# Moving transposes and row sums behind the value matmuls in a two-block diffusion transformer kernel

## The chip, the core and the metric

The kernel runs on one core of a Trainium2 chip. The metric is the device time of one execution in microseconds; the median of three runs is given. One further execution was taken with the hardware profiler. Engines are named as in the profile: PE is the matmul engine, PEld its weight loads, DVE, ACT and POOL the vector, scalar and general engines, SP the engine that issues most DMAs.

## The reference, cut to what matters

Everything is float32. Eight samples of 512 tokens with 256 features pass through two transformer blocks. Block 0 has 16 heads of 16 features and no projections in its self-attention:

```python
h = modulate(ln(x), shift_sa, scale_sa)
q = ln(_heads(h, H)) * qn_w + qn_b
k = ln(_heads(h, H)) * kn_w + kn_b
v = _heads(h, H)
attn = jax.nn.softmax(jnp.einsum('bhqd,bhkd->bhqk', q, k) * scale, axis=-1)
x = x + gate_sa[:, None, :] * _unheads(jnp.einsum('bhqk,bhkd->bhqd', attn, v))
```

A cross-attention over 64 context tokens and a gated feed-forward (256 to 1024 and back) follow. Block 1 has 16 heads of 64 features, with projections `wq`, `wkv`, `wo`, rotary positions on queries and keys, then a cross-attention over the same context and a GELU feed-forward:

```python
attn_in = _adaln(x, cond, ln1_w, ln1_b, g1_w, g1_b, b1_w, b1_b)
x = _attn(attn_in, attn_in, sa_wq, sa_wkv, sa_wo, sa_bo) + x
cross_in = _adaln(x, cond, ln1_w, ln1_b, g1_w, g1_b, b1_w, b1_b)
x = _attn(cross_in, ctx_n, ca_wq, ca_wkv, ca_wo, ca_bo) + x
x = gelu(ffn_in @ ff_w1 + ff_b1) @ ff_w2 + ff_b2 + x
```

## The kernel before, in words

**Order.** Inside the two stages that the change touches, the order of instructions on PE, DVE, ACT and POOL is the order in which the program writes them (a manual schedule). Semaphores between engines follow from the tiles. So "behind the values" means: later in the program, and later on each engine's queue.

**Block 0.** `run_blocks` walks a list of blocks, 18 for each sample (`CYCLE = H + 2`). In a sample's cycle, 16 blocks are self-attention: four head groups `g`, each with four key tiles `kt`; the two others (places `X0 = 11` and `X1 = 13`) are the previous sample's cross-attention. A block has scores (four matmuls on four 32-row strips of PE, into two tiles of `bank_s`, then two exponentials on ACT, L590) and values (four matmuls on four 32-column strips; plain values of a self-attention block go to `ps_O`). From block 18 on, blocks come in pairs. For the pair (i, i+1) the loop writes:

```python
scores(i)
others(i - 2); others(i - 1)
scores(i + 1)
values(i - 1); values(i)
```

`others` runs what was filed under a block's number in `beside` with `at(i, fn)`; below, it is called the middle. Filed there are:
- `queries_keys(g)` (L564 on): four 128x128 transposes of the normed heads `z` into one bank (L570), copied to `q` by ACT (L573) and to `k` by DVE (L574); filed 4 blocks before the group's first scores (2 in the first cycle).
- `group_end(g)`: ACT copies `ps_O` to `oT` (L603). `group_back(g)`: four transposes of `oT` into one bank (L610); DVE reads the denominators, inverts them and multiplies (L617 to L619); POOL multiplies by the gate and adds to x (L621, L622).
- `turn` of `batch2` (cross-attention) and of `batch3` (feed-forward): `transposed` (L427, L428) writes eight transposes into two banks, and ACT turns each into half of `hT`.
- The feed-forward's `up` (two matmul pairs into two banks; tanh on ACT L779; two DVE operations L780, L781) and `down`, the cross-attention's queries and its output projection, and the norms (DVE, with powers on POOL).

Turns of the feed-forward are collected in a list `later` and filed last, so that they come behind the other work of the same block number. All matmul outputs of the middle take a bank from `bank_x`, which in block 0 rotates over three banks (two of `ps_X` and `ps_D`). Each PE matmul of the program is two in the trace [...]; a transpose is one.

**Block 1's self-attention.** `slots` walks slots `m`, each with two blocks of 32-row scores. A slot writes: scores of block 2m+1; the jobs of `steps[m]`, the middle again, with the entry of `mid[m]` put in at place 1; scores of block 2m+2; values of blocks 2m and 2m+1 (64-column matmuls into `ps_O` and `ps_D`); then the list `after[m]`. A sample has eight slots: four head groups of four key tiles. `bank_x` rotates over two banks here. Jobs in the middle are projections for queries and keys (two banks each, rotated by DVE L999, L1000 and added on POOL L1002, L1003), for values (two banks, copied by ACT L989), the output projection `out_tiles` (one bank, added to x by DVE L464), and `turn` of the next sample.

The softmax denominators: POOL and DVE add the exponentials of a head group (L1035, L1039) into `sm`; `sums(g)` reduces `sm` with four 32-column matmuls by `ones32` into one bank, ACT copies it to `den` (L1055), DMAs carry it to DRAM and back reshaped into `rec`; `inverse(g)` is a DVE reciprocal (L1067) and two more DMA steps that broadcast it into `rb`; `scaled(g)` is two POOL products `oT * rb` (L1085). With n = 8b + 2g + 2, `sums` is in the middle of slot n (`mid[n]`), `inverse` in `after[n]`, `scaled` last in the middle of slot n+1. `out_tiles(0)` and `out_tiles(1)` come first in the middles of slots 8b + 10 and 8b + 11. The next sample's `turn` is the last job of the slot that holds the sums of g = 1.

Of the kernel before, what the change touches and what calls it, by code (L numbers as in the profile page):

```python
# [17 lines left out]
B, N, D, H, T, CD, FF = 8, 512, 256, 16, 64, 192, 1024  # L18
# [30 lines left out]
        self.scores, self.values = scores, values  # L49


def run_blocks(blocks, beside, alone):

    def scores(i):
        for fn in blocks[i].scores if i < len(blocks) else []:
            fn()

    def values(i):
        for fn in blocks[i].values if 0 <= i < len(blocks) else []:
            fn()

    def others(i):
        for fn in beside.get(i, []):
            fn()

    others(-1)
    for i in range(alone):  # L70
        scores(i)
        values(i - 1)
        others(i)
    scores(alone)
    values(alone - 1)
    for i in range(alone + 1, max(len(blocks) + 2, *(k + 3 for k in beside)), 2):
        scores(i)
        if i > alone + 1:
            others(i - 2)
        others(i - 1)  # L80
        scores(i + 1)
        values(i - 1)
        values(i)


def fast_path(ctx: ExitStack, tc: tile.TileContext, a: dict, out: bass.AP):
# [394 lines left out]


    blocks = []
    beside = {}

    def at(i, fn):
        beside.setdefault(max(i, -1), []).append(fn)

    CYCLE = H + 2
    X0, X1 = 11, 13  # L490
# [2 lines left out]
    def batch1(b):  # L493
        s = {}
        base = CYCLE * b
# [128 lines left out]
        n = 0  # L624
        for g in range(4):
            for kt in range(NT):
                while n in (X0, X1):
                    n += 1
                i = base + n
                blocks[i] = block(g, kt)  # L630
                if g == 0 and kt == 0:
                    if b == 0:
                        def before():
                            for n in range(3):
                                norm(n)
                            nc.vector.tensor_copy(qk_cols, cols[:, 0:2])
                            for fn in (first_modulated, head_centre, head_square, head_var):
                                fn(0, 0)
                            head_scale(0, 0, nc.vector)

                        at(-1, before)
                        at(0, lambda: awake(3))
                        for k, par, fns in ((0, 1, (first_modulated, head_centre)),
                                            (1, 1, (head_square, head_var, head_scale)), (2, None, (first_modulated,)),
                                            (3, None, (head_centre,)), (4, None, (head_square, head_var, head_scale))):
                            for fn in fns:
                                at(k, lambda fn=fn, par=par: fn(0 if par else 1, par))
                        at(5, lambda: spread(s["gate"], b, G_SA, D))
                    else:

                        for m, k in enumerate((-11, -10, -9) if b == 1 else (-13, -12, -10)):
                            at(i + k, lambda m=m: norm(m))
                        for c in range(2):
                            for k, fn in zip((-6, -5, -5, -4) if b == 1 else (-7, -5, -3, -3) if c else (-9, -8, -7, -7),
                                             (head_centre, head_square, head_var, head_scale)):
                                at(i + k, lambda c=c, fn=fn: fn(c))
                if kt == 0:
                    at(i - (2 if i <= CYCLE else 4), lambda g=g: queries_keys(g))
                if kt == NT - 1:
                    at(i + 1, lambda g=g: group_end(g))  # L660
                    at(i + 2 + (b > 0 and n % 2 == 0), lambda g=g: group_back(g))
                n += 1


    def batch2(b):
        s = {}
        base = CYCLE * (b + 1)
# [67 lines left out]

        for n, i in enumerate((2, 2, 3)):
            at(base + i, lambda n=n: prepare(n))
        at(base + 5, turn)
        at(base + 7, lambda: queries(0))
        at(base + 8, lambda: queries(1))  # L740
        end = b == B - 1
# [9 lines left out]
    def batch3(b):  # L751
        s = {}

        base = CYCLE * (b + 2) + {B - 3: 4, B - 2: 3, B - 1: -2}.get(b, 0)

        def prepare(n):

            if n == 0:
                s["gate"] = gate = wk3.tile([P, D], F32, tag="gate3", name="gate3")
                spread(gate, b, G_FF, D)  # L760
                s["pieces"] = normed_in_pieces(wk2, b, EPS0, lambda z: s.update(z=z))
            s["pieces"][n]()

        def turn():
            s["hT"] = transposed(wk2, s["z"], b, modT[:, 6:8, :], modT[:, 4:6, :])

        def up(f):
            if f == 0:
                s["hid"] = wk3.tile([P, 8, N], F32, tag="hid", name="hid", bufs=1)
            fs = slice(f * P, (f + 1) * P)  # L770
            pss = []
            for w in (w_1, w_3):
                ps = bank_x()
                for k in range(2):
                    mm(ps, w[:, k, fs], s["hT"][:, k, :], k == 0, k == 1)
                pss.append(ps)

            t = wk3.tile([P, N], F32, tag="t", name="t")
            nc.scalar.activation(t, pss[0], AF.Tanh, scale=0.5)  # L779
            nc.vector.scalar_tensor_tensor(t, t, 1.0, pss[0], ALU.add, ALU.mult)  # L780
            nc.vector.tensor_tensor(s["hid"][:, f, :], pss[1], t, ALU.mult)  # L781

        def down(t):
            ps = bank_x()[:, 0:D]
            project_tile(ps, 0, lambda k: s["hid"][:, k, :], w_2, 8, t)
            tmp = wk2.tile([P, 2, D], F32, tag="tmp", name="tmp", bufs=1)[:, 0, :]
            nc.vector.tensor_tensor(tmp, ps, s["gate"], ALU.mult)
            x = xs[b][:, t, :]
            nc.vector.tensor_tensor(x, x, tmp, ALU.add)

        places = {B - 2: (3, 3, 5, 6, 8), B - 1: (2, 2, 2, 4, 7)}.get(b, (4, 4, 6, 8, 9))
        for n in range(3):
            at(base + places[n], lambda n=n: prepare(n))
        later.append((base + places[3], turn))
        for f in range(8):
            at(base + places[4] + f, lambda f=f: up(f))
        for t in range(4):
            at(base + places[4] + 8 + (t if b > B - 3 else 2 * t), lambda t=t: down(t))

    blocks = [Block([], []) for _ in range(CYCLE * (B + 2))]  # L800
# [120 lines left out]
    later = []  # L921
    for b in range(B):
        batch2(b)
        batch3(b)
    for i, fn in later:
        at(i, fn)
    run_blocks(blocks, beside, CYCLE)
    ms.close()
    l0.close()

# [34 lines left out]
    with tc.tile_pool(name="ph4", bufs=2) as wk:  # L965
# [5 lines left out]
        def last(slot, fn):  # L971
            steps.setdefault(slot, []).append(fn)

        def batch4(b):
# [115 lines left out]
            if b:  # L1090

                pieces = normed_in_pieces(nk, b, EPS1, lambda z: s.update(z=z))
                last(base - 8, pieces[0])
                last(base - 6, pieces[1])
                after[base - 6] = [pieces[2]]
                last(base - 5, lambda: add_row(b, row("sabo")))
                last(base - 4, turn)
                last(base - 3, lambda: queries(0))
                last(base - 2, lambda: values(0, (0, 1)))
                last(base - 2, lambda: keys(0))  # L1100
                last(base - 1, lambda: values(0, (2, 3)))
            else:
                s["hT"] = ready

                def begin():
                    queries(0)
                    add_row(0, row("sabo"))
                    both = bank_s()
                    keys(0, (both[:, 0, :], both[:, 1, :]))
                    values(0, (0, 1))  # L1110
                    values(0, (2, 3))

                last(-1, begin)
                last(4, lambda: [nc.gpsimd.memset(z, 0.0) for z in (kb, vb)])
                last(5, lambda: load_kb(0))
# [9 lines left out]
        for b, (score, value, sums, inverse, scaled, out_tiles, _) in enumerate(todo):  # L1125
            base = 2 * NG * b
            for g in range(NG):
                if b == B - 1 and g == NG - 1:
                    break
                n = base + 2 * g + 2  # L1130
                mid[n] = lambda g=g, f=sums: f(g)
                after.setdefault(n, []).append(lambda g=g, f=inverse: f(g))
                last(n + 1, lambda g=g, f=scaled: f(g))
            if b < B - 1:
                for qp in range(2):
                    steps[base + 2 * NG + 2 + qp].insert(0, lambda qp=qp, f=out_tiles: f(qp))

        def slots():
            n = B * NG * NT
# [1129 lines left out]
```

## Time and profile before

| | us |
|---|---|
| Runs: median (lowest to highest of 3) | 2404.46 (2400.79 to 2407.53) |
| Profiled execution, its own time | 2400.53 |
| Its span, from first to last instruction | 2398.4 |
| PE busy | 2373.4 (99%) |
| PEld, DVE, ACT, POOL busy | 1160.7, 1138.7, 890.6, 967.9 |
| Start of block 1's self-attention slots | about 866 |
| One cycle of block 0 (18 blocks), e.g. 316.8 to 402.2 | 85 |
| One sample of block 1's self-attention, e.g. 1244.2 to 1366.8 | 122.5 |

The granted clock of PE was 0.998 of full speed. Busy time is from an instruction's start to its end, and instructions of an engine can overlap, so mean durations are longer than the distance from start to start. A timeline row merges instructions of one line and tile that follow without a gap; "x8" is their number; what stands in brackets is the idle time before the row and who ended it.

### The profile page before, as it was taken

The page shows a single profiled execution, that of the slowest core. Times are in us where ns is not written, and L with a number is a line of the kernel's source. Part 1 is how long each engine was busy: PE and PEld are TensorE (multiplying, and loading weights), DVE is VectorE, ACT ScalarE, POOL GpSimd, SP SyncE. Part 2 cuts the span into 40 slices and gives each one's busy share as a digit, 9 for nine tenths or more (in the row PEclk, how much of TensorE's full clock was granted, in tenths as well). Part 3 has the DMA queues.
Part 4 walks back from the last instruction along what each step waited for, and adds up shares of the span by engine and source line. Part 5 has one row for each costly group of instructions (what it writes and reads, how often), then busy time and mean ns, then how long its engine had stood idle before and what let it go on. Part 6 is the DMA issues. An engine that isn't in the chain of part 4 may idle for free.

```text
span 2398.4 us, 28561 instructions
## 1 busy us (share of the span) xinstructions
PE 2373.4 (99%) x10964; PEld 1160.7 (48%) x10964; DVE 1138.7 (47%) x2115; ACT 890.6 (37%) x1118; POOL 967.9 (40%) x588
## 2 busy tenths in 40 slices
PE   9999999999999999999999999999999999999998
PEld 4333544544545633444444444444445566667665
DVE  4564534434335345554545464645435767651110
ACT  4665545555542134333333333333332222221221
POOL 4563223323201046554646455555553544541110
PEclk9999999999999999999999999999999999999999
DMA  5130000000002001000000000000113222210000
GB/s 185 33 108 11 16 15 9 17 16 7 13 11 92 1 1 32 10 28 10 28 10 19 19 19 19 19 19 19 36 55 106 69 69 69 65 56 31 18 22 20
DMA packets 84897, 84.07 MB, mean 35 GB/s; under 512 B 42656, under 2 KB 59792, under 8 KB 84752
## 3 DMA queue, kind: packets, MB, share of 16 engines
q1 hardware_dynamic: 83208, 78.99, 10.7%
q8 instruction: 88, 1.44, 0.2%
q0 software_dynamic: 640, 2.10, 0.2%
q10 hardware_dynamic: 904, 1.07, 0.1%
q14 instruction: 57, 0.47, 0.1%
HBM read 72.09 MB, written 10.04 MB: 34 GB/s over the span
## 4 chain that ended last, share of the span: by engine, by line
PE 90%; DVE 4%; issue 3%; POOL 1%; ACT 1%; DMA 1%; SPq 0%; DVEq 0%; POOLq 0%; ACTq 0%
PE ps_X L116 37%; PE ps_S L116 23%; PE ps_D L116 15%; PE ps_O L116 13%; DVE sm L1039 1%; PE ps_X L427 1%; DMA rb<-rec 1%; ACT p L590 0%; PE ps_X L610 0%; DVE t L1000 0%; POOL var L561 0%; DVE t L999 0%; DVE t L843 0%; DVE z L215 0%; PE ps_X L570 0%
## 5 line engine op out<-in xcount | busy, mean ns | idle before, releaser
L116 PE MATMUL ps_S<-q,k 32*128 32x512 f32 (+1 forms) x3072 | 425.8, 623 | 5.5 <-ACT p L590 3.4
L1020 ACT ACTIVATE p<-ps_S 128x1024 f32<-128x1024 f32 x256 | 250.9, 1023 | 459.5 <-PE ps_S L116 450.2
L590 ACT ACTIVATE p<-ps_S 128x1024 f32<-128x1024 f32 x256 | 248.4, 1022 | 171.5 <-PE ps_S L116 170.2
L116 PEld LDWEIGHTS ps_S<-q,k 32*128 32x128 f32 (+1 forms) x3072 | 148.7, 183 | 244.6 <-issue 155.3
L1039 DVE TENSOR_TENSOR sm<-sm,p 128x1024 f32<-128x1024 f32 x128 | 252.0, 2027 | 0.1
L999 DVE TENSOR_TENSOR t<-ps_X,rope_c 128x512 f32<-128x512 f32 x126 | 87.0, 690 | 341.7 <-PE ps_X L116 341.7
L1002 POOL TENSOR_TENSOR q<-t 128x512 f32<-128x512 f32 x32 | 65.6, 2051 | 294.4 <-DVE t L1000 294.4
L182 POOL TENSOR_TENSOR rstd<-rstd,mhalf 128x4 f32<-128x4 f32 x49 | 51.2, 1045 | 292.7 <-DVE rstd L181 291.8
L844 POOL TENSOR_TENSOR q<-t,t 128x512 f32<-128x512 f32 x72 | 95.1, 1320 | 159.6 <-DVE t L843 159.6
L116 PE MATMUL ps_X<-hT,w 128*128 128x512 f32 x328 | 151.3, 597 | 0.5 <-DVE t L780 0.5
L1035 POOL TENSOR_TENSOR sm<-p 128x1024 f32<-128x1024 f32 x64 | 149.5, 2358 | 1.7 <-ACT p L1020 1.7
L1085 POOL TENSOR_TENSOR oT<-oT,rb 128x512 f32<-128x512 f32 x63 | 129.0, 2065 | 19.4 <-DMA rb<-rec_d 19.4
L116 PE MATMUL ps_O<-p,v 128*64 128x512 f32 x512 | 134.9, 605 | 0.0
L116 PE MATMUL ps_D<-p,v 128*64 128x512 f32 x512 | 131.6, 592 | 0.0
L116 PE MATMUL ps_O<-p,h 128*32 128x512 f32 x1024 | 129.4, 609 | 0.6 <-ACT p L590 0.6
L621 POOL TENSOR_TENSOR attn<-attn,gate 128x256 f32<-128x256 f32 x32 | 23.3, 728 | 250.7 <-DVE attn L619 250.7
L1002 POOL TENSOR_TENSOR k<-t 128x512 f32<-128x512 f32 x32 | 40.7, 1273 | 192.6 <-DVE t L1000 192.6
L116 PE MATMUL ps_X<-w_sa_wv,hT 128*128 128x512 f32 x256 | 118.0, 604 | 0.0
L116 PE MATMUL ps_X<-hT,w_sa_wq 128*128 128x512 f32 x256 | 115.9, 595 | 0.0
L116 PE MATMUL ps_X<-w_sa_wo,oT 128*128 128x256 f32 x512 | 114.5, 382 | 0.1
L116 PE MATMUL ps_X<-hT,w_sa_wk 128*128 128x512 f32 x248 | 114.6, 605 | 0.0
L116 PE MATMUL ps_S<-hT,w_ff_w 128*128 128x512 f32 x256 | 111.3, 592 | 0.0
(285 smaller groups left out, 3659.9 us busy)
## 6 DMA issues: line engine op xcount, KB each, us to landing
rb<-rec SPq DMA_DIRECT2D x128, 128.0 KB
rb<-rec_d SPq DMA_DIRECT2D x124, 128.0 KB
rb<-rec SPq DMA_DIRECT2D x16, 256.0 KB
out_dram<-x SPq DMA_DIRECT2D x15, 256.0 KB
x<-in_x_dram SPq DMA_DIRECT2D x7, 512.0 KB
gate<-modd SPq DMA_DIRECT2D x24, 128.0 KB
k_d<-q POOLq DMA_DIRECT2D x8, 256.0 KB, 2.4
v_d<-v SPq DMA_DIRECT2D x8, 256.0 KB
```

The lines of the kernel that those rows point to most:

```text
L116: nc.tensor.matmul(o, lhsT, rhs, start=start, stop=stop)
L182: nc.gpsimd.tensor_tensor(r[:, :n], r[:, :n], mhalf[:, :n], ALU.pow)
L427: nc.tensor.transpose(ps[:, t * P : (t + 1) * P], z[:, t, k * P : (k + 1) * P], ident)
L590: nc.scalar.activation(pr[u], pss[u], AF.Exp, scale=HD0 ** -0.5)
L621: nc.gpsimd.tensor_tensor(attn, attn, gate.to_broadcast([P, NT, 4, HD0]), ALU.mult)
L844: nc.gpsimd.tensor_tensor(dst, t1, t2, ALU.add)
L999: nc.vector.tensor_tensor(c, ps, rope_c, ALU.mult)
L1002: nc.gpsimd.tensor_tensor(r[0], ec, os, ALU.subtract)
L1020: nc.scalar.activation(pr, pss[u], AF.Exp, scale=HD1 ** -0.5)
L1035: nc.gpsimd.tensor_tensor(sm, s["p", g, 0, u], s["p", g, 1, u], ALU.add)
L1039: nc.vector.tensor_tensor(s["sm", g, u], s["sm", g, u], s["p", g, t, u], ALU.add)
L1085: eng.tensor_tensor(o, o, s["rb", g, u], ALU.mult)
```

## The change

1. `run_blocks` takes a second set of filed work, `behind`, which runs after the pair's values, for the same block numbers as the middle.
2. `then(i, fn)` files in `behind` where 45 <= i < 129 (`2 * CYCLE + 9` to `CYCLE * (B - 1) + 3`), and in `beside` otherwise. `queries_keys`, `group_back`, `batch2`'s `turn` and, up to sample B - 3, `batch3`'s `turn` are filed with it. In the full cycles `group_back` is filed 1 block after its group's last block (4 for g = 2) instead of 2 or 3, `batch2`'s `turn` at place 6 instead of 5, and the last piece of `batch3`'s norm at place 7 instead of 6.
3. In block 1's self-attention, for all samples but the last, `sums` goes to the front of `after[n]`, `inverse` to `mid[n + 1]`, `scaled` to `after[n + 1]`; the next sample's `turn` goes to `after` as well; `out_tiles(0)` becomes the second job of its slot.

```diff
-def run_blocks(blocks, beside, alone):
+def run_blocks(blocks, beside, behind, alone):
...
-    for i in range(alone + 1, max(len(blocks) + 2, *(k + 3 for k in beside)), 2):
+    for i in range(alone + 1, max(len(blocks) + 2, *(k + 3 for k in (*beside, *behind))), 2):
...
         values(i - 1)
         values(i)
+        for fn in (*behind.get(i - 2, []), *behind.get(i - 1, [])):
+            fn()
...
+    def then(i, fn):
+
+        (behind if 2 * CYCLE + 9 <= i < CYCLE * (B - 1) + 3 else beside).setdefault(max(i, -1), []).append(fn)
...
-                    at(i - (2 if i <= CYCLE else 4), lambda g=g: queries_keys(g))
+                    then(i - (2 if i <= CYCLE else 4), lambda g=g: queries_keys(g))
                 if kt == NT - 1:
                     at(i + 1, lambda g=g: group_end(g))
-                    at(i + 2 + (b > 0 and n % 2 == 0), lambda g=g: group_back(g))
+                    full = 2 * CYCLE + 9 <= i < CYCLE * (B - 1)
+                    then(i + ((4 if g == 2 else 1) if full else 2 + (b > 0 and n % 2 == 0)), lambda g=g: group_back(g))
...
-        at(base + 5, turn)
+        then(base + (6 if 1 < b < B - 2 else 5), turn)
...
-        places = {B - 2: (3, 3, 5, 6, 8), B - 1: (2, 2, 2, 4, 7)}.get(b, (4, 4, 6, 8, 9))
+        places = {B - 2: (3, 3, 5, 6, 8), B - 1: (2, 2, 2, 4, 7)}.get(b, (4, 4, 7 if 0 < b < B - 3 else 6, 8, 9))
...
-        later.append((base + places[3], turn))
+        later.append((at if b > B - 3 else then, base + places[3], turn))
...
-    for i, fn in later:
-        at(i, fn)
-    run_blocks(blocks, beside, CYCLE)
+    for put, i, fn in later:
+        put(i, fn)
+    run_blocks(blocks, beside, behind, CYCLE)
...
-                last(base - 4, turn)
+                after.setdefault(base - 4, []).append(turn)
...
-                mid[n] = lambda g=g, f=sums: f(g)
-                after.setdefault(n, []).append(lambda g=g, f=inverse: f(g))
-                last(n + 1, lambda g=g, f=scaled: f(g))
+                if b == B - 1:
+                    mid[n] = lambda g=g, f=sums: f(g)
+                    after.setdefault(n, []).append(lambda g=g, f=inverse: f(g))
+                    last(n + 1, lambda g=g, f=scaled: f(g))
+                else:
+                    after.setdefault(n, []).insert(0, lambda g=g, f=sums: f(g))
+                    mid[n + 1] = lambda g=g, f=inverse: f(g)
+                    after.setdefault(n + 1, []).append(lambda g=g, f=scaled: f(g))
             if b < B - 1:
                 for qp in range(2):
-                    steps[base + 2 * NG + 2 + qp].insert(0, lambda qp=qp, f=out_tiles: f(qp))
+                    steps[base + 2 * NG + 2 + qp].insert(1 - qp, lambda qp=qp, f=out_tiles: f(qp))
```

More of the change, by code (lines that the diff above doesn't have):

```diff
@@ L483, in fast_path @@
     blocks = []
-    beside = {}
+    beside, behind = {}, {}
     def at(i, fn):
         beside.setdefault(max(i, -1), []).append(fn)
+    def then(i, fn):
+        (behind if 2 * CYCLE + 9 <= i < CYCLE * (B - 1) + 3 else beside).setdefault(max(i, -1), []).append(fn)
     CYCLE = H + 2
```

## The prediction, made before the changed kernel was run

> **What bounds the kernel now.** I read the page first (busy shares and the chain), then the waits of PE, then PE's timeline in three stretches, together with the weight loads (PEld) and ACT in one of them. All durations below run from one start to the next start of PE groups, because the ends of matmuls are modelled.
>
> ```profile
> span 2398.4 us, 28561 instructions
> PE 2373.4 (99%) x10964; PEld 1160.7 (48%) x10964; DVE 1138.7 (47%) x2115; ACT 890.6 (37%) x1118; POOL 967.9 (40%) x588
> PE 90%; DVE 4%; issue 3%; POOL 1%; ACT 1%; DMA 1%; SPq 0%; DVEq 0%; POOLq 0%; ACTq 0%
> ```
>
> PE is busy 99% of the span and carries 90% of the chain: only what shortens PE's own queue shortens the kernel, and nearly all of what does so shows in the end. But a matmul that waits behind its weight load still counts as a busy PE, so I looked for stalls inside busy time.
>
> ```profile
> PE ps_X L116 <- DVE t L1000: 2.2, 6, 0.4
> PE ps_X L116 <- DVE sm L1039: 1.8, 1, 1.8
> ...
> PE ps_D L116 <- DVE t L780: 0.7, 3, 0.3
> ...
> PE ps_X L116 <- DVE t L780: 0.5, 3, 0.2
> ```
>
> Open waits of PE are small (line waited for: us in total, times, longest). The list of weight loads adds the hidden ones:
>
> ```profile
> PEld ps_S L116 <- ACT p L590: 53.3, 70, 2.5
> ```
>
> Seventy times the weights of block 0's scores wait for an exponential of ACT. One pair of blocks shows what it costs (start, length, engine and line; first PE, then ACT, then the weight loads from 363.905 on):
>
> ```profile
> 360.15 0.60 PE L570 MATMUL ps_D<-ident,z 128*128 128x128 f32 x4
> 360.68 1.14 PE L116 MATMUL ps_S<-q,k 16*128 16x512 f32 x8
> 361.75 1.92 PE L116 MATMUL ps_O<-p,h 128*32 128x512 f32 x16
> 363.61 1.43 PE L116 MATMUL ps_S<-q,k 16*128 16x512 f32 x8
> 364.97 0.66 PE L610 MATMUL ps_X<-ident,oT 128*128 128x128 f32 x4
> 365.46 0.38 PE L116 MATMUL ps_X<-w,hid 128*128 128x256 f32 x1
> ```
> ```profile
> 361.92 1.94 ACT L590 ACTIVATE p<-ps_S 128x1024 f32<-128x1024 f32 x2 [0.35 <-PE ps_S L116]
> ```
> ```profile
> 363.91 0.30 PEld L116 LDWEIGHTS ps_S<-q,k 16*128 16x128 f32 x4
> ```
>
> Scores after a transpose take 1.07 us (360.68 to 361.75), scores straight after values 1.36 (363.61 to 364.97). The two exponentials of the scores before end at 361.92 + 1.94 = 363.86, and the second half's weights start at 363.91: the values (1.86) are too short to cover ACT. The stall is 0.29 us, and every score group straight after plain values has it: all 31 of the timeline between 270 and 760 us took 1.357 to 1.362.
>
> Block 1 has no such stall (its values take 3.58, its scores 1.93 everywhere), but its sums sit in the middle of full-array matmuls:
>
> ```profile
> 1244.17 7.17 PE L116 MATMUL ps_X<-w_sa_wo,oT 128*128 128x256 f32 x32
> 1251.27 1.06 PE L116 MATMUL ps_X<-sm,ones 128*32 128x512 f32 x8
> 1252.27 3.70 PE L116 MATMUL ps_X<-hT,w_sa_wk 128*128 128x512 f32 x8
> ```
> ```profile
> 1281.32 3.70 PE L116 MATMUL ps_X<-hT,w_sa_wk 128*128 128x512 f32 x8
> 1285.39 1.07 PE L116 MATMUL ps_X<-sm,ones 128*32 128x512 f32 x8 [0.37 <-DVE t L1000]
> 1286.59 1.23 PE L427 MATMUL ps_X<-ident,z 128*128 128x128 f32 x8
> 1287.75 2.00 PE L116 MATMUL ps_S<-q,k 32*128 32x512 f32 x16
> ```
>
> The tile shape (128*128, 128*32, 32*128) changes at every group border; in the second stretch sums and transposes also wait for a bank that DVE is still rotating out of.
>
> [...] 128x512 matmuls of one shape start 0.43 us apart, at a change of shape 0.52, so 0.09 per change; the first full-array matmul after a change costs 0.10 more (16 up-matmuls take 7.06 after scores, 6.96 after transposes), a first transpose 0.06. [...] exponentials, copies and evacuations run in program order. So what a move puts ahead of an exponential or of a bank's evacuation counts.
>
> **The change, part by part.**
>
> *Block 0, transposes behind the values.* Over the full cycles the order of PE shows 54 banks of four transposes moved: 32 groups behind values, 14 of one bank, 14 of two, 4 of three. Removed from the middle: 19 that came first there (0.49 each, of which 0.10 passes to the matmul that now comes first: 0.39), 9 last, 10 between up-matmuls (4 x 0.109 = 0.44 each), 8 pairs (0.87): 7.4 + 4.0 + 4.4 + 7.0 = 22.8 us. Added behind: 0.49 for the first bank, 0.44 for each more, 0.09 for the change back to scores: 14 x 0.59 + 14 x 1.02 + 4 x 1.46 = 28.4 us. So the extra shape changes cost +5.6. Score groups straight after plain values fall from 51 to 24: 27 stalls of 0.287 go, -7.7, as even one bank (0.59) outlasts 0.29. The up-matmuls' waits for DVE (L780, 0.7 + 0.5) go, -1.2. Five groups stand behind a cross-attention's values, where scores take 1.07 already; they pay and gain nothing (counted). Sum: -3.3 us.
>
> Does the middle become too short? Scores are free for the next ones 3.2 us after they start (360.68 to 363.86); 1.07 of scores plus the shortest middle left (two query or one down projection, 3.65) is 4.7. No stall. What is queued on ACT behind the moved transposes: the copy of q (0.78) or of hT (1.45 for two) now stands ahead of the next exponentials. It starts 0.64 after a bank's first transpose (360.15 to 360.79); with three banks it ends at 0.49 + 0.58 + 1.45 = 2.5 us after the group's start, and the exponential is due at 1.46 + 1.23 = 2.7. Nothing late, with 0.2 to spare. On DVE the head's evacuation (denominator, reciprocal, product) moves behind the middle's jobs; it ended 1.6 us after the transposes' start in the cycle shown, and with three banks its bank is needed at 1.46 + 1.07 = 2.5. POOL's two products (0.73 each) for the third group move behind a power of 5.44 and a 1.06 product; only the next group's product waits for them, some 8 us later. SP's queue is in the same order in both kernels.
>
> *Block 1, sums behind the values.* 28 sums move, and the six later pairs of turn transposes with the first one too. By the kind of slot: 6 with an output projection and 14 with two projections: the group goes from a middle of 8.26 (or 11.73) to 7.06 (10.54, as the same jobs take without a sum) plus 1.00 behind: -0.20 each, -4.0. One with keys alone: equal. Seven with keys, sum and turn: six had 6.43 from 1281.32 to 1287.75 and will have 3.63 + 1.00 + 1.02 + a new wait. The new wait: with two banks, the turn's second transposes need the sum's bank, which ACT's copy of den frees 1.72 after the sum's start (1285.39 to 1287.11), where they are due at 1.49: 0.28. So 5.93, -0.5 each, -3.0. The first (910.78 to 920.23, 9.45) loses its waits of 1.81 and 0.87 as well: -3.5. Sum: -10.5 us.
>
> Behind these: the reciprocal moves to the next slot's middle, behind its first job on DVE. Its operand landed 5.0 us after the sum's start (1285.39 to 1290.38), so 4.0 after the next slot begins; scores and one job take 5.5. POOL's products come one slot later in the program but behind the same rotations as before, and the broadcast lands about 6 us after the reciprocal; the last group's is needed by an output projection that itself moves behind the keys (3.6 later). I cost these at nothing; with the cover gone, POOL's wait would be that of before (19.4 us in three waits) and reach PE only through the rotated keys behind it.
>
> *Sum*: -3.3 - 10.5 = -13.8 us. The profiled execution took 2400.5 us, 2.1 over its span: 2386.7 for such an execution. It lies 3.9 under the median of the runs shown, 2404.46; taken over unchanged, 2404.5 - 13.8 = 2390.7.
>
> Not shown before: values followed by transposes in full cycles. The same change of shape elsewhere costs 0.09, and transposes behind sums started 0.29 late, of which 0.20 was a bank; so 0 to 0.2 more per group, 0 to +6.4 in all. A gain below 0.09 is excluded by every change in the trace. I take 0. The 0.28 at the turns may be absent (-2.0).
>
> **Rivals.** (1) The 0.29 is the change of shape, not ACT, and stays: -13.8 + 7.7, 2398.4. Against it: cross-attention values have the same shape and the scores behind them take 1.07. (2) The waits removed in block 1 come back at the new places, since DVE's sums (7.9 us in a run) are as long as before: the -6.5 of the seven turn slots is lost, 2397.2. Against it: the sums end 3.7 us into the slot (1245.97 against 1242.24), the moved matmuls come at 9. (3) Slower: a bank held too long. Every moved group takes one to three of the three banks just before the next middle needs them, while DVE, in order, still works at the middle's norms; one centring (0.68 + 0.18 + 1.17) ahead of the evacuation makes it 1.1 us late. At 32 groups that is +35, 2426. It decides the sign from 0.43 us a group. For it: DVE's runs there are long. Against it: only the four groups of three banks hand the evacuated bank straight to the next matmul. That the change doesn't move what it says is excluded by the order of the instructions.
>
> **How the numbers follow.** My forecast 0.76, rival 1 0.08, rival 2 0.10, rival 3 0.06. About 0.3% (7.2 us, below 2397.2) is what a measurement of this kernel can tell from no change. Faster: the forecast, half of rival 2 and a little of rival 1, less the forecast's slow tail: 0.81; same 0.13; slower 0.06. Range: down by the absent turn wait and the runs' own spread (3.4), to 2385.5; up by the bound of the new border, which takes in rivals 1 and 2, to 2398.5.
>
> **What would show it.** Scores behind plain values and transposes at 1.07; the wait of PEld for L590 falling from 70 times to some 45; no wait for the sums, turn slots at about 5.9 and projection slots at 8.06. Wrong, if PE waits at ps_X or ps_D for DVE after the moved groups, or exponentials start later than 1.23 us after their scores.

## The result, and the profile after

| | before | after |
|---|---|---|
| Median (lowest to highest) of 7 runs each, us | 2405.21 (2400.79 to 2409.96) | 2395.76 (2387.34 to 2396.04) |
| Profiled execution, its own time, us | 2400.53 | 2395.50 |
| Its span, us | 2398.4 | 2393.4 |

The ratio is 0.9949, with a 95% interval of 0.9935 to 0.9963: faster by 0.5%. The seven runs of after lie on two levels, 2387.3 and 2389.1 at a granted clock of PE of 0.998 and 0.997, and five from 2395.5 to 2396.0 at 0.994 to 0.995. What the change itself did and what the clock did have to be told apart.

The page of after, in the order in which before was read:

```profile
span 2393.4 us, 28547 instructions
PE 2369.5 (99%) x10964; PEld 1156.6 (48%) x10964; DVE 1140.9 (48%) x2115; ACT 887.8 (37%) x1118; POOL 960.2 (40%) x588
PE 94%; DVE 2%; POOL 1%; issue 1%; DMA 1%; ACT 1%; SPq 0%; POOLq 0%; DVEq 0%; ACTq 0%
```

PE still is the bound, with the same 10964 matmuls, and has more of the chain than before (94% against 90%). The waits of PE (line waited for: us in total, times, longest):

```profile
PE ps_D L576 <- POOL z L568: 3.6, 2, 3.1
...
PE ps_X L118 <- DVE t L850: 1.7, 1, 1.7
...
PE ps_X L118 <- DVE t L1007: 0.5, 1, 0.5
PE ps_D L118 <- DVE t L787: 0.3, 1, 0.3
```

The rotation's wait (L1000 before, L1007 here) is down from 2.2 us in six to 0.5 in one, the wait of 1.8 for `sm` is gone, and the up-matmuls' (L780 before, L787 here) is down from 1.2 to 0.3. Two new ones stand at the top: 3.1 us for POOL in the opening, and 1.7 for a rotation of the second cross-attention (L850, 0.5 before). The weight loads of block 0's scores wait 39 times for an exponential, where they waited 70 times (some 45 were forecast):

```profile
PEld ps_S L118 <- ACT p L596: 29.8, 39, 2.5
```

PE's timeline (start, length, engine, line, operation), at the pair of blocks that the prediction showed:

```profile
368.00 1.92 PE L118 MATMUL ps_O<-p,h 128*32 128x512 f32 x16
369.86 0.66 PE L616 MATMUL ps_D<-ident,oT 128*128 128x128 f32 x4
370.35 0.60 PE L576 MATMUL ps_X<-ident,z 128*128 128x128 f32 x4
370.88 1.14 PE L118 MATMUL ps_S<-q,k 16*128 16x512 f32 x8
371.95 2.21 PE L118 MATMUL ps_X<-w,hid 128*128 128x256 f32 x9
```

Two banks behind the values take 1.02 us (369.86 to 370.88), and the scores after them 1.07 (to 371.95) instead of 1.36. And a turn slot of block 1:

```profile
1287.08 1.07 PE L118 MATMUL ps_X<-sm,ones 128*32 128x512 f32 x8
1288.07 1.44 PE L429 MATMUL ps_X<-ident,z 128*128 128x128 f32 x8
1289.44 2.00 PE L118 MATMUL ps_S<-q,k 32*128 32x512 f32 x16
```

Sum and turn now follow the values, in 2.36 us; eight transposes take 1.37 there. The prediction counted 1.02 for them and 0.28 for the new wait for the sum's bank; the wait is 0.35.

**Where the time went.** Consecutive scores of PE form 312 groups in both kernels, so one can measure from the start of one group to that of another. The table gives such distances, in us, in the two profiles:

| stretch (groups, counted from 0) | before | after | difference |
|---|---|---|---|
| 0 to 45, opening | 172.29 | 180.00 | +7.71 |
| 45 to 143, block 0's full cycles | 551.32 | 546.19 | -5.13 |
| 144 to 277, block 1's self-attention and the start of its cross-attention | 1039.10 | 1029.62 | -9.48 |
| 143 to 144 and 277 to 278, the borders | 96.55 + 6.96 | 95.88 + 8.18 | -0.67, +1.22 |
| 278 to 311, the rest | 479.40 | 479.40 | 0.00 |

The two stretches that the change touches give -14.6. The opening takes 7.7 of them back, and in it PE's instructions stand in the same order in both kernels. First a place in before, then the same place and a later one in after:

```profile
71.51 2.78 PE L116 MATMUL ps_S<-q,k 16*128 16x512 f32 x8 [2.06 <-ACT p L590]
```
```profile
72.30 2.04 PE L118 MATMUL ps_S<-q,k 16*128 16x512 f32 x8 [2.05 <-ACT p L596]
...
82.55 1.11 PE L576 MATMUL ps_D<-ident,z 128*128 128x128 f32 x4 [3.08 <-POOL z L568]
...
84.87 2.09 PE L118 MATMUL ps_S<-q,k 16*128 16x512 f32 x8
86.89 1.94 PE L118 MATMUL ps_O<-p,h 128*32 128x512 f32 x8
```

Behind an idle time of 3.08 us in after, scores take 2.02 instead of 1.07 and values 1.87 for half their usual number: PE runs at half clock, by the clock's records from 82.1 to 102.6 us (granted clock 0.50). Before had 6.8 us of that, from 72.7 to 79.5, behind its idle time of 2.06 us, and both have another 3.4 us between 158 and 171. The experiments had to show whether this belongs to the change.

### The profile page after: what moved, and what is told of

It reads as the page before. It is cut to its first block, busy times and chain, and to the rows that moved or that the text cites. A ratio compares the mean times of both kernels' runs of the same rounds, so it can differ in the third digit from the quotient of the medians.

```text
span 2393.4 us, 28547 instructions
## 1 busy us (share of the span) xinstructions
PE 2369.5 (99%) x10964; PEld 1156.6 (48%) x10964; DVE 1140.9 (48%) x2115; ACT 887.8 (37%) x1118; POOL 960.2 (40%) x588
## 3 DMA queue, kind: packets, MB, share of 16 engines
q1 hardware_dynamic: 83208, 78.99, 10.6%
q10 hardware_dynamic: 904, 1.07, 0.1%
## 4 chain that ended last, share of the span: by engine, by line
PE 94%; DVE 2%; POOL 1%; issue 1%; DMA 1%; ACT 1%; SPq 0%; POOLq 0%; DVEq 0%; ACTq 0%
PE ps_X L118 39%; PE ps_S L118 24%; PE ps_D L118 15%; PE ps_O L118 14%; PE ps_X L429 1%; POOL var L567 1%; DMA rb<-rec 1%; PE ps_X L616 0%; PE ps_X L576 0%; DVE t L850 0%; DMA rec<-rec 0%; PE ps_D L576 0%; PE ps_D L429 0%; PE ps_D L616 0%; ACT p L596 0%
## 5 line engine op out<-in xcount | busy, mean ns | idle before, releaser
L118 PEld LDWEIGHTS ps_S<-q,k 32*128 32x128 f32 (+1 forms) x3072 | 143.0, 185 | 231.9 <-issue 162.5
L1009 POOL TENSOR_TENSOR q<-t 128x512 f32<-128x512 f32 x32 | 59.7, 1866 | 331.3 <-DVE t L1007 290.2
L567 POOL TENSOR_TENSOR var<-var,mhalf 128x32 f32<-128x32 f32 (+1 forms) x17 | 87.3, 5137 | 159.0 <-DVE var L561 158.9
L466 DVE TENSOR_TENSOR x<-ps_X,x 128x512 f32<-128x512 f32 x27 | 18.7, 691 | 195.6 <-PE ps_X L118 195.6
```

The costliest lines, as they stand in the source:

```text
L118: nc.tensor.matmul(o, lhsT, rhs, start=start, stop=stop)
L567: nc.gpsimd.tensor_tensor(var, var, half, ALU.pow)
L1009: nc.gpsimd.tensor_tensor(r[0], ec, os, ALU.subtract)
```

## The experiments

**Filling PE's idle time in the opening.** The half-clock records of the opening last 3.413, 6.827 and 20.480 us: one, two and six times 3.413. The two long ones stand beside idle times of PE: in before the idle time of 2.06 us ends at 71.51 and the record starts at 72.68; in after the one of 3.08 ends at 82.55 and the record starts at 82.10. After's idle time of 2.05 us, up to 72.30, has no record beside it. That the idle time brings the fall about is my guess from the two cases; what decides between 2.06 with a fall and 2.05 without one is not shown. So unused transposes fill PE's idle time; nothing reads their banks, and what is computed stays the same.

```diff
+    def fill(n):
+        ps = bank_x()
+        for _ in range(n):
+            mm(ps[:, 0:P], ident, ident)
...
+    at(14, lambda: fill(8))
+    beside.setdefault(16, []).insert(0, lambda: fill(13))
+    beside.setdefault(16, []).insert(0, lambda: fill(1))
```

In the kernel before:

> The kernel before, with unused transposes of the identity put where PE stood idle in the opening (8 behind block 14's place, 14 ahead of block 16's transposes), so that PE does not fall to half clock there; what is computed is unchanged. My theory: the half-clock records of the opening (6.83 us in before, 20.48 us in after) come from PE's idle time there and have nothing to do with the change. Then no half-clock record is left in 60 to 110 us and this kernel takes 2397 to 2400 us. Rival: the clock's fall is not set by PE's idle time; the records stay and the time is that of before, 2401 to 2407.

In the changed kernel:

> The changed kernel with the same unused transposes in the opening. My theory: the change is worth -13 to -14 us at an equal clock and 7.7 us of it were lost to the opening's lower clock in most runs; so 13 to 14 us under before_awake, 2384 to 2387 us, and its runs no longer fall on two levels 7 us apart. Rival: the loss in the opening belongs to the change (its layout of code or buffers); then it stays 20 us at half clock, about 2394, and only some 6 under before_awake.

Measured: 2405.65 us (2400.18 to 2411.15, 22 runs) and 2392.40 (2386.20 to 2394.01, 6 runs), beside 2407.03 for the kernel before on the same chip. Both expectations missed on the level: the half-clock records at 72.7 us (before) and 82.1 us (after) were gone from the profiles, but the other runs still lie on levels. before_awake's median lies where its rival had put it, and its ratio to the kernel before, 0.9998 (0.9988 to 1.0007), shows no gain from this filler. after_awake is 13.2 us under before_awake, as the theory said, and not 6. Read by each run's granted clock (before_awake's times at 0.999 and 0.997 lie 4.3 us apart, so a step of 0.001 is about 2 us and the differences are no finer than that), they tell more:

| granted clock | before_awake, us (runs) | after_awake, us (runs) | difference |
|---|---|---|---|
| 0.999 | 2401.57 (8) | 2386.69 (2) | -14.9 |
| 0.997 | 2405.90 (7) | 2392.40 (2) | -13.5 |
| 0.996 | 2406.94 (1) | 2392.87 (1) | -14.1 |
| 0.995 | 2410.36 (5) | 2394.01 (1) | -16.4 |

At one clock the change is worth 13.5 to 16.4 us, and a kernel's runs differ by 7 to 9 us with the clock. The same holds without any filler: 46 runs of the kernel before on that chip average 2410.98 at 0.994 (4 runs), 2410.08 at 0.995 (14), 2403.63 at 0.997 (10) and 2401.78 at 0.998 (4), and after's own 2395.77, 2395.93, 2389.05 and 2387.34 are 15.2, 14.2, 14.6 and 14.4 below.

**Each part alone,** with the same filler. Block 1's edits undone:

```diff
-                after.setdefault(base - 4, []).append(turn)
+                last(base - 4, turn)
...
+                mid[n] = lambda g=g, f=sums: f(g)
+                after.setdefault(n, []).append(lambda g=g, f=inverse: f(g))
+                last(n + 1, lambda g=g, f=scaled: f(g))
...
```

> The block 0 part of the change alone (transposes behind the values), with the same unused transposes in the opening. My reading of the changed kernel's profile: -5.8 us against before_awake, of which -7.8 is 27 stalls of scores. The prediction on record: -3.3. Rival (the parts depend on each other, block 0's gain is in part block 1's): below -2 or above zero.

And block 0's edits undone (no `behind`, everything filed in `beside` at the places of before):

> The block 1 part of the change alone (sums and turns behind the values), with the same unused transposes in the opening. My reading of the changed kernel's profile: -9.4 us against before_awake (first turn -3.5, six turns -2.8, 18 projections about -0.2 each, +0.5 at the last sample). The prediction on record: -10.5. If the 1.2 us more at the second cross-attention's wait (L850) belong to this part they are lost here as well: -8.2 instead of -9.4.

Measured: 2396.02 and 2392.40 us at a clock of 0.999 (5 and 4 runs), 5.6 and 9.2 under before_awake's 2401.57. In the stretches they are exact (one profile each): block 0's part alone takes 546.19 and 1039.08, block 1's alone 551.30 and 1029.61. The parts add up, and neither leans on the other. My -5.8 had counted the border from 143 to 144, which lies anywhere from 95.9 to 97.3 in 13 profiles and not by kernel; so it is -5.1. The border from 277 to 278 is either 6.95 or 8.18, with and without either part of the change (6.95 in before, after_awake, before_thin and after_warm, 8.18 in the nine others): the 1.2 us at L850 are not the change's. What decides between the two stays open.

block0_awake's own profile fell on a low clock (0.997), and tells why filling one place wasn't enough: half clock from 92.1 to 99.0 and from 102.4 to 105.8, later than the filler. PE is hardly idle ahead of either (one gap of 0.59 us), but its scores take 1.6 us twice before the first and 2.2 at the second instead of 1.07, as their weights wait for exponentials. before_awake has the same scores of 1.6 us at this place, and there the clock stays full (0.999 over the run; scores at 100.65 take 1.07). So thin stretches like these follow each other through the opening; what decides on which of them the clock falls is not shown.

**The price of transposes between up-matmuls.** The block 0 step missed by 1.8 us. In before's timeline a wait follows the transposes that stand between up-matmuls:

```profile
316.02 0.60 PE L570 MATMUL ps_D<-ident,z 128*128 128x128 f32 x4
316.79 3.70 PE L116 MATMUL ps_X<-hT,w 128*128 128x512 f32 x8 [0.17 <-DVE t L780]
320.42 1.14 PE L116 MATMUL ps_S<-q,k 16*128 16x512 f32 x8
```

From the four transposes to the next matmul it takes 0.77 us here, and 0.50 in five of the ten cases, not 4 x 0.109 = 0.44; the eight matmuls behind them take 3.63, and eight that follow without a break 3.53. All such transposes are those of queries and keys. So only these were moved, all else of block 0 as before:

```diff
-                    then(i + ((4 if g == 2 else 1) if full else 2 + (b > 0 and n % 2 == 0)), lambda g=g: group_back(g))
+                    at(i + 2 + (b > 0 and n % 2 == 0), lambda g=g: group_back(g))
...
-        then(base + (6 if 1 < b < B - 2 else 5), turn)
+        at(base + 5, turn)
...
-        places = {B - 2: (3, 3, 5, 6, 8), B - 1: (2, 2, 2, 4, 7)}.get(b, (4, 4, 7 if 0 < b < B - 3 else 6, 8, 9))
+        places = {B - 2: (3, 3, 5, 6, 8), B - 1: (2, 2, 2, 4, 7)}.get(b, (4, 4, 6, 8, 9))
...
-        later.append((at if b > B - 3 else then, base + places[3], turn))
+        later.append((at, base + places[3], turn))
```

> Of block 0's part only the transposes of queries and keys move behind the values; oT's and the turns' stay in the middle. By the order of the instructions 14 of 27 stalls go (14 x 0.287 = -4.0), 19 banks stand behind values (19 x 0.59 = +11.2) and leave the middle, 9 of them last there (0.44 each), 10 between up-matmuls. The step on record (0.44 each for those ten, and 1.2 for their waits) gives -4.0 + 11.2 - 4.0 - 5.6 = -2.4 us. My reading of the changed kernel's profile (0.61 for each of the ten without a wait, 0.88 with one, half and half) gives -4.2. Read from the stretch between the score groups 45 and 143, which took 551.3 us before and 546.2 with all of block 0's part.

And the complement:

```diff
-                    then(i - (2 if i <= CYCLE else 4), lambda g=g: queries_keys(g))
+                    at(i - (2 if i <= CYCLE else 4), lambda g=g: queries_keys(g))
```

> The complement: only oT's and the turns' transposes move behind the values, 35 banks in 23 groups. 22 stalls go (-6.3); behind values 15 x 0.59 + 4 x 1.02 + 4 x 1.46 = +18.7; out of the middle 19 that came first (0.39 each) and 16 later ones (0.44), -14.4. Both the prices on record and my reading give -2.0 us in the stretch that took 551.3. If it gains well over 2.0, the error of the block 0 step is not in the transposes between up-matmuls.

Measured in the stretch, one run each: 547.12, -4.2, as the new price says (the recorded one said -2.4), and 548.46, -2.8 (expected -2.0). So the error of the step lies in these ten interruptions. What it consists of, the complement shows: there the ten stay, and cost 0.8 us less. One of them in before (PE with its weight loads, then DVE):

```profile
291.58 0.60 PE L570 MATMUL ps_X<-ident,z 128*128 128x128 f32 x4
292.08 0.30 PEld L116 LDWEIGHTS ps_D<-hT,w 128*128 128x128 f32 x2
292.08 1.98 PE L116 MATMUL ps_D<-hT,w 128*128 128x512 f32 x4
```
```profile
288.84 0.42 DVE L619 TENSOR_TENSOR attn<-ps_X,inv 128x256 f32<-128x256 f32 x1
...
290.26 1.17 DVE L544 TENSOR_TENSOR z<-h,mean 128x512 f32<-128x512 f32 x1
291.35 0.68 DVE L780 SCALAR_TENSOR_TENSOR t<-t,ps_D 128x512 f32<-128x512 f32 x1
```

And the same place in the complement:

```profile
296.54 0.60 PE L582 MATMUL ps_X<-ident,z 128*128 128x128 f32 x4
296.87 0.30 PEld L118 LDWEIGHTS ps_D<-hT,w 128*128 128x128 f32 x2
296.98 1.88 PE L118 MATMUL ps_D<-hT,w 128*128 128x512 f32 x4
```
```profile
295.65 0.69 DVE L793 SCALAR_TENSOR_TENSOR t<-t,ps_D 128x512 f32<-128x512 f32 x1 [0.70 <-ACT t L792]
```

The bank that the next up-matmuls write, here `ps_D`, is one that DVE reads at L780. In before this read comes behind the head's evacuation (L617 to L619) and a centring (L542 to L544). It ends at 291.35 + 0.68 = 292.03, the weights follow at 292.08, and the matmul starts with them, 0.50 after the transposes. In the complement the evacuation stands behind the values and the centring runs earlier. The read (L793) ends at 296.34, before the transposes start, so the weights load during the last of them, and the matmul starts after 0.44, which is 4 x 0.109. So it goes in five of the ten places; in the other five DVE's read ends at 0.72 after the transposes' start, and the matmul starts at 0.77, in both kernels. In all 15 cases in which the weights wait, they start 0.05 after the read ends, and the first matmul behind them takes 0.10 more; where they don't wait, nothing is added. So the transposes' own price was right at this place too. What was too small are the waits behind them: 5 x 0.06 + 5 x 0.33 + 10 x 0.10 = 3.0 us, where the prediction had counted the open waits of PE, 1.2. The difference is the 1.8.

**Is the stall of 0.29 ACT's, or the change of shape's?** One unused matmul of 32 columns was put behind 37 plain values of the kernel before; it takes PE's time and adds the second change of shape, but gives ACT time too.

```diff
         values(i - 1)
         values(i)
+        if 45 <= i < 143 and not {i % alone, (i - 1) % alone} & {11, 13}:
+            thin()
...
+    run_blocks(blocks, beside, CYCLE, lambda: mm(bank_x()[:, 0:32], ident, ident[:, 0:32]))
```

> The kernel before (with the unused transposes in the opening) and one unused matmul of 32 columns behind the plain values of 37 pairs of blocks in the full cycles, into a bank that nobody reads. Its two passes and the two changes of shape should take about 0.2 us. If the 0.29 us of scores behind values is ACT's exponential (the prediction), they fit into that time and the stretch of 551.3 us grows by 0 to 1 us. If it is the change of shape (rival 1), each costs its whole time: +7 us or more.

PE's timeline, and then the weight loads' wait for ACT in the same kernel:

```profile
368.01 1.92 PE L118 MATMUL ps_O<-p,h 128*32 128x512 f32 x16
369.87 0.41 PE L118 MATMUL ps_X<-ident 128*128 128x32 f32 x2
370.20 1.14 PE L118 MATMUL ps_S<-q,k 16*128 16x512 f32 x8
```
```profile
PEld ps_S L118 <- ACT p L598: 18.5, 30, 1.1
```

The extra matmul takes 0.34 from its start to the scores' (more than the 0.2 that I expected), and the scores go down to 1.07. In this one run 36 of them lie in the stretch: 36 x 0.338 = 12.2 us of added work made it 1.87 us longer (551.30 to 553.17). 37 score groups there lose their stall, 10.6 of the 12.2; the rest of the difference, 0.2, is in transposes of z. So added work up to the length of the stall was free here; a stall from any change of shape would have cost the whole 12.2. One that belonged to the direct step from values (128*32) to scores (16*128) alone would have gone as well, but in before six score groups make this very step behind a cross-attention's values, and take 1.07. Rival 1 is out.

**One clock for both kernels.** More filler, at every place of the opening where scores wait for exponentials. In after_warm_tail the output projection that stands in the last sample's slot (it is that of the sample before) also goes back to the front: in after, this slot's order is keys' matmuls, sums, projection, and the projection waits for a bank that DVE still reads:

```profile
1728.73 1.88 PE L118 MATMUL ps_X<-hT,w_sa_wk 128*128 128x512 f32 x4
1730.54 1.06 PE L118 MATMUL ps_X<-sm,ones 128*32 128x512 f32 x8
1732.05 3.29 PE L118 MATMUL ps_X<-w_sa_wo,oT 128*128 128x256 f32 x14 [0.45 <-DVE t L1007]
```

```diff
+    for i, n in ((3, 3), (6, 3), (8, 4), (17, 3), (18, 4), (20, 6), (36, 5), (40, 5)):
+        beside.setdefault(i, []).append(lambda n=n: fill(n))
+    beside[2].insert(0, lambda: fill(5))
...
-                    steps[base + 2 * NG + 2 + qp].insert(1 - qp, lambda qp=qp, f=out_tiles: f(qp))
+                    steps[base + 2 * NG + 2 + qp].insert(1 - qp if b < B - 2 else 0, lambda qp=qp, f=out_tiles: f(qp))
```

> The changed kernel with more unused transposes in the opening (38 more, wherever PE's weights wait for an exponential between 25 and 110 us and at 155 and 171 us), and with the last sample's output projection first in its slot again as in the kernel before, so that its sums don't meet a bank that DVE still holds. Theory: [...] with all of them covered every run shows 0.999 and takes 2385 to 2387.5 us, at a spread under 3 us. Rival: the runs still fall on levels from 2386 to 2395 us. The slot of the last sample should lose its wait of 0.45 us.

The filler alone, in the kernel before and in the changed one:

> The kernel before with all the unused transposes in the opening that kept the clock at 0.999 to 1.0 in the last run, to compare the change at one clock. Theory (the levels of the times are the clock's): every run at 0.999 or above, 2400 to 2402 us, at a spread under 3 us. Rival (the clock held by chance, or by the change): the runs spread over 2400 to 2411 us as before.

> The changed kernel with the same unused transposes in the opening, nothing else. The stretches that the change touches gave -5.1 (block 0) and -9.5 us (block 1) in every profile so far: 14.6 us under before_warm, 2386 to 2388 us. The prediction on record: 13.8 under. The rival that runs slower by chance of the clock: 7 to 22 under, by luck.

Measured (median, lowest to highest, runs; ratio to the kernel before on the same chip with its 95% interval):

| | us | ratio |
|---|---|---|
| before_warm | 2402.38 (2400.40 to 2404.12, 22) | 0.9984 (0.9977 to 0.9991) |
| after_warm | 2387.46 (2386.07 to 2388.78, 6) | 0.9928 (0.9911 to 0.9945) |
| after_warm_tail | 2386.06 (2384.74 to 2387.38, 6) | 0.9913 (0.9895 to 0.9930) |

All 34 runs show a clock of 0.998 to 1.0, and the levels are gone: the runs of a kernel now lie within 2.6 to 3.7 us (a little more than the 3 expected), where those of the kernel before lie within 11.5 beside them (2400.72 to 2412.22). In the profiles no half-clock record is left but one at the very end. The stretch from 60 to 130 us (PE, PEld, DVE, ACT, POOL busy, granted clock, share and rate of the DMAs), in after and then in before_warm:

```profile
60.00:130.00 70.00, 63.23 (x334) 23.44 (x337) 33.93 (x98) 37.30 (x43) 32.16 (x21) 0.85 0.10 28
```
```profile
60.00:130.00 70.00, 68.51 (x445) 31.65 (x444) 37.68 (x108) 41.28 (x48) 37.84 (x26) 1.00 0.10 29
```

At one clock the change is worth 2402.38 - 2387.46 = 14.9 us, and its stretches -5.1 (551.29 to 546.18) and -9.5 (1039.10 to 1029.61), as in every profile. The opening (groups 0 to 45) now takes 171.95 us in before_warm and 171.94 in after_warm, where it took 172.29 and 180.00 without filler: the 7.7 us that after lost there are the clock's, not the change's. The tail edit took 0.5 off its stretch (1029.09). after_warm_tail beats both kernels; most of its lead over after is the clock's.

**Sums or turns?** after_warm_tail with block 1's turns back in the middle:

```diff
-                after.setdefault(base - 4, []).append(turn)
+                last(base - 4, turn)
```

> after_warm_tail with block 1's turns left in the middle, last in their slots, as in the kernel before; the sums stay behind the values. Which of the two moves makes the turn slots shorter? If it is the sums' (my view: with turns in the middle they meet the bank that DVE rotates out of, 0.37, in place of the wait of 0.28 to 0.35 for the sums' bank behind the values), the stretch between the groups 144 and 277 stays within 1 us of 1029.1. If the turns' move gives the 0.5 per slot that the prediction put on the pair, it is 3 us or more longer.

Measured (one run): 1038.76 in the stretch, 9.7 longer, and only 0.3 under before's 1039.10. My expectation failed. A turn slot of this kernel:

```profile
1278.41 0.66 PE L435 MATMUL ps_X<-ident,z 128*128 128x128 f32 x4 [0.37 <-DVE t L1019]
1279.93 0.66 PE L435 MATMUL ps_X<-ident,z 128*128 128x128 f32 x4 [0.87 <-ACT hT L436]
1280.52 2.00 PE L118 MATMUL ps_S<-q,k 32*128 32x512 f32 x16
```

Both halves of the turn now wait: the first 0.37 for DVE's rotation, as foreseen, and the second 0.87 more, until ACT's copy of the first half ends (0.78 from 1279.10), which I had not foreseen. In before the sum stood between keys and turn; it took the first wait, and the turn waited 0.2 us at most. Now these slots are 0.75 longer than in before (six times) and the first, from which the sum's own waits have gone, 0.9 shorter: +3.6. The other 20 slots give their -3.9 all the same. So moving the sums alone gains 0.3 us, and moving the turns with them makes of the seven slots' loss of 3.6 a gain of 6.1.

## Why the prediction was right, and where it was off

The forecast, faster with 2390.7 us in a range from 2385.5 to 2398.5, holds: 2395.76. By its own steps, in the two stretches, in which no profile has a half-clock record (us, rounded one by one):

| step | forecast | measured |
|---|---|---|
| 27 stalls of scores in block 0 | -7.7 | -7.8 |
| block 0's transposes moved, with the up-matmuls' waits | +4.4 | +2.6 |
| 20 sums behind the values | -4.0 | -3.9 |
| the first turn slot | -3.5 | -3.5 |
| six turn slots | -3.0 | -2.6 |
| output projection behind the sums, in the last sample's slot | none | +0.5 |
| sum | -13.8 | -14.6 |

- **The stalls** are right in mechanism, number and size. The scores' column of the stretch went from 117.32 to 109.55 us, and the thin matmul, with the weights' recorded waits for ACT, shows that ACT is the cause.
- **The moved transposes** were mis-sized in one term: the up-matmuls' waits, "(L780, 0.7 + 0.5) go, -1.2". The prediction had looked for stalls inside busy time and found them at the scores' weights; here it counted only the waits that show as idle time of PE. With the late weights the waits at the ten interruptions come to 3.0. Their transposes' own 0.44 each was right, as were the added prices, 0.59, 1.02 and 1.46 for one to three banks, to 0.01.
- **"I take 0"** for the unseen border from values to transposes was right: 0.587 with four transposes, where 0.59 was forecast.
- **The turn slots**: 5.93 was forecast and 5.99 measured; the wait for the bank is 0.35 instead of 0.28. The pair was costed rightly, but the text didn't see that the sum had been covering the turn's waits in before, so that the gain there stands or falls with both moves.
- **The last sample's slot** was missed: it has keys, sums, projection, since `out_tiles(0)` and the sums both go to place 1. Reading only slots of the middle samples hid it; 0.5 us.
- **Rival 2** (waits that come back) happened once, for 0.45 us, and **rival 3** not at all: none of the moved groups waits for a bank in block 0, as the list of waits shows.
- **The level**: the errors in the two blocks nearly cancel, and yet the median is 5 us above the forecast. The failing step is "taken over unchanged": taking 13.8 from a median of 2404.46 took the mixture of clocks for a constant. Five of seven runs of after fell on its lower clock, which costs 7 to 8 us; at like clock the differences are 14.2 to 15.2. That the levels are the clock's is shown by the warm kernels. Why five of seven, and not half, fell on the low one is open: chance is enough, and nothing here shows a share of the change in it. That 2395.76 still lies within the range is luck: its upper end allowed 0 to 6.4 us for the new border, which cost nothing, and that room took up the 5 us of the clock, for which no term stood. (The lower end's own terms, 2390.7 - 2.0 - 3.4, give 2385.3, and the upper one's, 2390.7 + 6.4, give 2397.1; the stated ends differ a little, and nothing hangs on it.)

## What to carry to other kernels

Look for stalls inside busy time: compare one group's length behind different predecessors, and if it differs by what another engine still has to do, put work of at least that length in between; up to the stall's length it was free here. Price a short group at its place: its own time followed from its repetition rate here, but the waits behind it must be read from the starts of the weight loads as well as from PE's idle time, since a late weight load need not show as idle. Before you move a group, ask what it covered where it stood, as the sums did for the turns. And compare kernels at the same granted clock: a thin opening can cost time by the clock alone (180.00 us in after, 171.94 with filler), and useless matmuls in PE's idle time there took 3.8 us off the median of the kernel before (2406.19 to 2402.38).

## What the runs showed of the hardware that was not expected

- Half clock came beside idle times of PE of 2.06 us (before) and 3.08 (after), and in block0_awake in a stretch with next to no idle time of PE in the records (one gap of 0.59 us), where only weights were late. In the openings of before and after the records last 3.41 us twice, 6.83 once and 20.48 once.
- Filling every thin place took the spread of the runs from 11.5 us to 3.7 and less. The fastest run hardly moved (2400.40 against 2400.72). Before's opening took 172.29 us with 10.2 us of half clock and 171.95 with none, and after's 180.00 with 23.9: by these figures half clock cost 0.3 us in the one case and 8.1 in the other. Why it cost so little in before is not shown.
- A distance of 551.3 or 1039.1 us between two groups repeats within 0.04 us from profile to profile, although the whole time varies by 10: a stretch bounded by PE's own queue is a much finer measure than the run.
- A matmul whose weights wait for a bank starts 0.05 us after DVE's read of it ends (15 cases), and the next one comes 0.53 instead of 0.43 us later. Neither need show as idle time of PE: waits of 0.06 us at five places are in no list of waits, and yet cost 0.17 each with the late start of the next matmul.
